# Layer 3 of a four-layer kernel: sums over states in four quarters of TensorE's array, and four of sixteen products du*B by TensorE

## The chip, the cores and the metric

The kernel runs on one core of a Trainium2 chip. Its time is the device time in microseconds of one execution, from the start to the end on that core. A core has five engines that run side by side, each with its own queue of instructions in a fixed order: TensorE (PE, matmuls from SBUF into PSUM), VectorE (DVE), ScalarE (ACT, activation functions), GpSimd (POOL) and SyncE (SP), which here issues nearly all DMAs.

## The reference, cut to what matters

Four layers work on eight images of 64 channels and 64 x 64 pixels. Layers 0 to 2 are not touched by the change. Layer 3 runs two directions of a Mamba block over one axis of the image, joins them by a linear map with a residual, and does the same over the other axis:

```python
def mamba1(x, nw, ipw, cw, cb, xpw, dtw, dtb, Alog, Dp, opw):
    xn = rms_norm(x, nw)
    xz = xn @ ipw.T                       # 64 -> 512
    xc, z = (xz[..., :d], xz[..., d:])    # d = 256
    xc = silu(causal_dwconv(xc, cw, cb))
    dbl = xc @ xpw.T                      # 256 -> 4 + 16 + 16
    dt = jax.nn.softplus(dbl[..., :r] @ dtw.T + dtb)
    Bm, Cm = dbl[..., r:r + n], dbl[..., r + n:r + 2 * n]
    A = -jnp.exp(Alog)
    y = selective_scan(xc, dt, Bm, Cm, A)
    return ((y + Dp * xc) * silu(z)) @ opw.T
# in selective_scan, for each step t of the sequence and each of n = 16 states:
    dA = jnp.exp(dt_t[:, :, None] * A)
    h = h * dA + (dt_t * x_t)[:, :, None] * B_t[:, None, :]
    y = jnp.einsum('bdn,bn->bd', h, C_t)
```

## The kernel before, in words

**Units and states.** Layer 3 is cut into 256 units: two axes (`s`), 16 chunks (`c`), four groups of eight sequences (`g`) and two directions (`k`; k=1 runs backwards). A unit has 512 tokens (eight sequences of 64). Its 256 channels lie as 128 partitions by two halves `j`, so that a tile is 128 x 1024 with the halves beside each other. For each of the 16 states n there is one pass over the tile. `stream` walks through all states of all units by one counter i (n = i modulo 16), and writes the order of every engine's queue out by hand: iteration i issues work for several states at once.

**What one state costs.** SP loads the rows of B and C of the state, spread over 128 partitions, into a tile `bc` six states ahead (L2068). POOL forms hb = du*B three states ahead (`multiply_b`, L484). ACT forms dA = exp(A*dt) in two halves two states ahead (`decay`, L491) into one of two PSUM tiles, in turn. DVE runs the scan h = dA*h + hb (`scan`, L500), in place in the PSUM tile of dA. Then h*C is formed (`multiply_c`, L514), for most states by DVE into a tile `hc`, for the states in the list `shared` by POOL, whose scan writes h to SBUF. PE adds the result to the unit's sum `acc` in PSUM, by matmuls with the identity (`gather`, L306), two iterations after the scan. `shared` has five states, or four in the k=1 units of odd g.

**Between units.** With state 0 of the next unit `gather` first lets DVE multiply the finished sum by z (`drain`, L2077), and PE then starts the next sum with D*u (`skip`, L2073). There is one tile `acc`. In iteration n=2 this stands behind the scan of state 2.

**Preparing the next unit.** `prepare` is a generator; `stream` runs one piece of it per iteration. Its pieces: PE forms px, the in-projection with the convolution's taps (L2012); ACT forms u = silu(px) (L2024); PE forms the 36 rows of dbl (L2027), ACT copies them out (L2030), SP stores the rows of B and C to HBM (L2033); PE forms dt's input (L2036), ACT dt = softplus (L415); POOL forms du = dt*u (L2047); PE forms z's input (L2050), ACT z = silu (L2060). Each matmul result stands in the PSUM tile `mm`, of which there is one (pool `pp`, one buffer), so that each waits for ACT to have read the one before.

**Other work in mm.** When both directions of a group are done, `finish` is queued as urgent: PE adds the residual and the four end products (L2096, L2099) in `mm`, and ACT copies them out (L2115). `begin` prepares a chunk of input, with the mean of squares in `mm`. `advance` runs their pieces where `room` allows it.

Of the kernel before, what the change touches and what calls it, by code (L numbers as in the profile page):

```python
# [10 lines left out]
F32 = mybir.dt.float32  # L11
# [7 lines left out]
C = 64  # L19
HW = 64  # L20
# [63 lines left out]
def twice(a):  # L84

    return np.concatenate([a, a], axis=0)
# [20 lines left out]
def layouts(i):  # L107
# [69 lines left out]
    o["l3_in"] = np.stack([twice(i[p + "in_proj_w"][k].T) for k in range(4)], axis=1)  # L177
# [6 lines left out]
    o["l3_xp"] = i[p + "x_proj_w"].reshape(4, 36, 2, 128).transpose(3, 0, 2, 1)  # L184
    o["l3_dtw"] = i[p + "dt_proj_w"].reshape(4, 256, 4).transpose(2, 0, 1)
# [3 lines left out]
    o["l3_out"] = i[p + "out_proj_w"].transpose(1, 0, 2)  # L189
# [73 lines left out]
def two(pool):  # L263


    return Ring([pool(f"pe{j}", 1, space=PSUM) for j in range(2)])


class Net:
# [33 lines left out]
    def mm(self, ps, lhsT, rhs, start=True, stop=True):  # L303

        for o, r in zip(blocks(like(ps, rhs)), blocks(rhs)):
            self.nc.tensor.matmul(o, lhsT, r, start=start, stop=stop)  # L306

# [124 lines left out]

    def stream(self, pools, ahead, steps, behind, rest=None):
# [30 lines left out]

        def fetch(i):
            if i < total and not isinstance(bp, tuple):
                s = steps[i // NS]
                t = bp.tile(s.bc_shape, F32, name="bc")
                s.load(i % NS, t)
                B[i], CC[i] = s.spread(t, 0), s.spread(t, 1)  # L470
            elif i < total:
                B[i] = bp[0].tile([128, T], F32, name="b")
                steps[i // NS].load(i % NS, 0, B[i])
# [5 lines left out]

        def multiply_b(i):  # L480
            if i < total:
                s = steps[i // NS]
                hb[i] = hbp.tile([128, T], F32, name="hb")
                nc.gpsimd.tensor_tensor(s.shaped(hb[i]), s.shaped(s.du), B.pop(i), ALU.mult)  # L484

        def decay(i):
            if i < total:
                s, n = steps[i // NS], i % NS
                dA[i] = pe.tile([128, T], F32, name="dA")
                for cut, A in s.lanes:  # L490
                    nc.scalar.activation(dA[i][:, cut], s.dt[:, cut], AF.Exp, scale=A[:, n : n + 1])  # L491

        def shared(i):
            return i % NS in steps[i // NS].shared

        def scan(i):
            s, n = steps[i // NS], i % NS
            h = hp.tile([128, T], F32, name="h") if shared(i) else dA[i]
            way = slice(None, None, -1) if s.rev else slice(None)
            nc.vector.tensor_tensor_scan(h[:, way], dA[i][:, way], hb.pop(i)[:, way], s.first(n), ALU.mult, ALU.add)  # L500
            dA[i] = h
            if shared(i):
                s.keep(n, h)

        def calm(i):

            return i + 1 >= total or not (shared(i) or shared(i + 1))
# [10 lines left out]
        def gather(i):  # L518
            at, n = divmod(i, NS)
            if n == 0:  # L520
                if at:
                    steps[at - 1].drain(acc.pop(at - 1))
                    steps[at - 1].done()
                acc[at] = pa.tile([128, T], F32, name="acc")
                begun[at] = steps[at].skip(acc[at])
            self.mm(acc[at], self.ident, hc.pop(i), start=n == 0 and not begun[at], stop=n == NS - 1)
# [12 lines left out]
        for i in range(total + 2):  # L539
            at, n = divmod(i, NS)  # L540
            need(i + ahead[0], "bc")
            need(i + ahead[1], "du")
            fetch_c(i + ahead[2])
            fetch(i + ahead[0])
            multiply_b(i + ahead[1])
            if 0 < i <= total and shared(i - 1):
                multiply_c(i - 1)


            first = i > NS and n == 2  # L550
            late = i > 1 and not first and steps[0].late and shared(i - 2)
            if i > 1 and not late and not first:
                gather(i - 2)
            if at + 1 < len(steps) and n == steps[at].start:
                steps[at + 1].ready()
                while self.held or self.urgent:
                    self.advance(behind)
                work = Task(steps[at + 1].prepare())
            if work is not None and not (self.held and work.said is None) and (calm(i) or not work.calm):
                work.step()  # L560
                if work.over:
                    work = None
            room = work is None or work.said is not True and (n < steps[0].early or hasattr(steps[at + 1], "du"))
            self.advance(behind, room, calm(i))
            if late:
                gather(i - 2)
            if i < total:
                scan(i)
            if first:
                gather(i - 2)  # L570
            if i < total:
                if not shared(i):
                    multiply_c(i)
            decay(i + 2)
# [292 lines left out]
    def layer1(self, src, dst):  # L867
        nc, tc, d = self.nc, self.tc, self.d
        mid = self.hbm["x1a"]
        with ExitStack() as ctx:  # L870
# [340 lines left out]
            class Step:  # L1211
                start, early, late = 2, 8, True
                shared = (1, 4, 7, 10, 13)
# [316 lines left out]
    def l2_scan(self, hx, hy):  # L1530
        nc, tc, d = self.nc, self.tc, self.d
        with ExitStack() as ctx:
# [36 lines left out]
            class Step:  # L1569
                bc_shape, start, early, late = [128, 2, T], 2, 0, False  # L1570
                shared = (1, 4, 7, 10, 13)
# [250 lines left out]
    def layer3(self, src, dst):  # L1822
# [8 lines left out]
        with ExitStack() as ctx:  # L1831
# [3 lines left out]
            pools = (pool("bc", 8), pool("hb", 4), pool("hc", 4), pool("h", 3), two(pool), pool("pa", 1, space=PSUM))  # L1835
            hp = pool("h3", 3, space=DRAM)
# [7 lines left out]
            class Weights:  # L1844
# [12 lines left out]
                def load(self):  # L1857
# [19 lines left out]
                    both = cp.tile([128, 2, 256], F32, name=f"both{s}")  # L1877
                    self.dtw, self.z = self.take("dtw", both[:4]), both[C:]
                    self.dtb, self.A, self.D = self.take("dtb"), self.take("A"), self.take("D")

                def build(self):
# [24 lines left out]
                    for k in range(2):  # L1906
                        nc.vector.tensor_scalar(
                            self.z[:, k, :], self.w_in[C:, k, 256:], self.nw[C:, k : k + 1], None, ALU.mult
                        )
# [14 lines left out]
            ends = [slice(3 + r, 3 + r + HW) for r in range(2)]  # L1924

# [58 lines left out]
            class Step:  # L1984
                bc_shape, start, early, late = [128, 2, W], 1, 0, False
# [5 lines left out]
                def __init__(self, s, c, g, k):  # L1991
                    self.s, self.c, self.g, self.k, self.rev = s, c, g, k, k == 1
                    self.w = weights[s]
                    self.shared = (2, 6, 10, 14) if k and g % 2 else (1, 4, 7, 10, 13)
                    self.lanes = [(slice(j * W, j * W + W), self.w.A[:, k, j, :]) for j in range(2)]
# [6 lines left out]
                def prepare(self):  # L2002
# [17 lines left out]
                    yield CALM  # L2020
# [4 lines left out]
                    pd = pp.tile([128, T], F32, name="mm")[:36, :W]  # L2025
# [3 lines left out]
                    dbl = p2.tile([36, W], F32, name="dbl")  # L2029
                    nc.scalar.copy(dbl, pd)  # L2030
                    self.bc = hp.tile([NS, 2, W], F32, name="bc")
                    for m in range(2):
                        nc.sync.dma_start(self.bc[:, m, :], dbl[4 + m * NS : 4 + m * NS + NS])  # L2033
                    pt = pp.tile([128, T], F32, name="mm")
                    for j in range(2):
                        nc.tensor.matmul(  # L2036
                            pt[:, j * W : j * W + W], w.dtw[:, k, j * 128 : j * 128 + 128], dbl[0:4], start=True, stop=True
                        )
                    yield True
                    yield CALM  # L2040
# [6 lines left out]
                    nc.gpsimd.tensor_tensor(du, dt, u, ALU.mult)  # L2047
                    pz = pp.tile([128, T], F32, name="mm")
                    for j in range(2):
                        nc.tensor.matmul(  # L2050
                            tokens(pz[:, j * W : j * W + W]),
                            w.z[:, k, j * 128 : j * 128 + 128],
                            xn[C:, :, 4 : 4 + HW],
                            start=True,
                            stop=True,
                        )
                    yield True
                    yield CALM
# [5 lines left out]
                    nc.scalar.copy(dt.rearrange("p (s t) -> p s t", t=HW)[:, :, at], endless)  # L2064

                def load(self, n, t):
                    row = self.bc[n : n + 1].rearrange("o m t -> o (m t)")
                    nc.sync.dma_start(t.rearrange("p m t -> p (m t)"), row.to_broadcast([128, 2 * W]))  # L2068

                def skip(self, acc):  # L2070
                    for j in range(2):
                        at = slice(j * W, j * W + W)
                        nc.tensor.matmul(acc[:, at], self.w.skip[self.k][:, j, :], self.u[:, at], start=True, stop=False)  # L2073
                    return True
# [83 lines left out]
```

## Time and profile before

| what | value |
|---|---|
| median of three runs | 24,507.96 us (24,494.8 to 24,517.75) |
| the profiled execution | 24,512.34 us, span 24,510.5 us, mean granted PE clock 0.939 |
| layer 3 in the profile | from 11,265 us to the end: 256 units, 51.7 us each |
| busy share, 20,000 to 24,000 us | PE 86%, DVE 97%, ACT 68%, POOL 99% |
| DMA busy share there | 0.52 of 16 engines |

A row of a group reads: line, engine, operation, output and inputs with shapes, count, then busy time in us and mean duration in ns, then idle time of the engine just before these instructions and what ended it. A row of the timeline reads: start, duration, engine, line, operation, count. Each f32 matmul shows as two records (two LDWEIGHTS and two MATMUL), in the timeline at 0.43 us from start to start for 512 columns at full clock. Durations of overlapping instructions overlap too, so start-to-start times are the ones that add up.

### The profile page before, as it was taken

The numbers are of one execution on the slowest core, as the hardware profiler recorded it, in microseconds if no ns is written. First come the engines' busy times: TensorE is split into PE (matmuls) and PEld (weight loads), VectorE is DVE, ScalarE is ACT, GpSimd is POOL, SyncE is SP. The second block draws the span as 40 slices with busy tenths as digits, with TensorE's granted clock in tenths as the row PEclk, the third lists the DMA queues.
The fourth block names the chain that finished last, engine by engine and source line by source line (L and its number), as shares of the span: only waits on it lengthen the run. The fifth ranks groups of instructions, "written<-read, shape, count | busy, mean of one in ns | idle before, by whom it ended". The sixth has DMA issues, their size and how long they took to land. (4 is left out here: it accounts for less than half of the span.)

```text
span 24510.5 us, 193203 instructions
## 1 busy us (share of the span) xinstructions
PE 20920.5 (85%) x53146; PEld 8078.3 (33%) x53146; DVE 22354.1 (91%) x13092; ACT 14737.2 (60%) x18960; POOL 22095.7 (90%) x10580
## 2 busy tenths in 40 slices
PE   7778888888888888898888888888888888888888
PEld 5323333333333223222333333333333333333333
DVE  5599999999998689978999999999999999999999
ACT  5445555555555456525666666666666666666666
POOL 0499999999999489967999999999999999999999
PEclk9889999999999999999999999999999999999999
DMA  3699889889888489924555555555555454555454
GB/s 78 203 327 321 312 313 322 314 313 320 313 313 309 171 287 339 317 54 121 172 169 172 170 172 169 170 170 172 170 170 173 169 174 167 173 170 172 168 174 157
DMA packets 1835294, 5282.70 MB, mean 216 GB/s; under 512 B 533712, under 2 KB 539924, under 8 KB 1831904
## 3 DMA queue, kind: packets, MB, share of 16 engines
q1 hardware_dynamic: 1809632, 5207.00, 62.8%
q10 hardware_dynamic: 24576, 63.33, 0.7%
q8 instruction: 423, 6.93, 0.1%
q14 instruction: 663, 5.43, 0.1%
HBM read 5112.85 MB, written 156.11 MB: 215 GB/s over the span
## 5 line engine op out<-in xcount | busy, mean ns | idle before, releaser
L484 POOL TENSOR_TENSOR hb<-du,bc 128x1024 f32<-128x1024 f32 x4608 | 10757.1, 2365 | 204.6 <-DVE h L500 144.3
L306 PE MATMUL acc<-hc,ident 128*128 128x512 f32 x18560 | 8783.6, 614 | 93.3 <-DVE img L1274 49.7
L491 ACT ACTIVATE dA<-dt,w_A 128x512 f32<-128x512 f32 x8192 | 5658.2, 691 | 3939.3 <-DVE hc L514 2886.0
L500 DVE TENSOR_TENSOR_SCAN dA<-dA,hb 128x1024 f32<-128x1024 f32 x3320 | 7579.3, 2283 | 195.4 <-ACT dA L491 105.2
L306 PE MATMUL acc<-h,ident 128*128 128x512 f32 x8064 | 4644.1, 705 | 2433.5 <-POOL h L514 2403.0
L306 PEld LDWEIGHTS acc<-hc,ident 128*128 128x128 f32 x18560 | 3639.8, 200 | 5218.0 <-issue 4534.5
L484 POOL TENSOR_TENSOR hb<-du,b 128x1024 f32<-128x1024 f32 x2048 | 4833.5, 2389 | 487.7 <-DVE dA L500 214.4
L514 DVE TENSOR_TENSOR hc<-dA,bc 128x1024 f32<-128x1024 f32 x3232 | 3956.5, 1224 | 246.0 <-issue 5.8
L491 ACT ACTIVATE dA<-dt,w_l_A 128x1024 f32<-128x1024 f32 x2560 | 2856.8, 1117 | 996.2 <-DVE hc L514 756.6
L500 DVE TENSOR_TENSOR_SCAN h<-dA,hb 128x1024 f32<-128x1024 f32 x1416 | 3228.9, 2280 | 79.9 <-ACT dA L491 77.8
L306 PEld LDWEIGHTS acc<-h,ident 128*128 128x128 f32 x8064 | 1565.6, 212 | 5153.0 <-POOL h L514 3477.1
L514 POOL TENSOR_TENSOR h<-h,bc 128x1024 f32<-128x1024 f32 x1376 | 3250.5, 2362 | 8.3 <-DVE h L500 8.3
L500 DVE TENSOR_TENSOR_SCAN dA<-dA,carry,hb 128x1024 f32<-128x1024 f32 x1320 | 3093.8, 2344 | 115.4 <-POOL hb L484 50.5
L514 DVE TENSOR_TENSOR hc<-dA,c 128x1024 f32<-128x1024 f32 x1408 | 1723.7, 1224 | 117.7 <-DMA c<-bc 5.1
L514 POOL TENSOR_TENSOR h<-h,c 128x1024 f32<-128x1024 f32 x640 | 1517.9, 2372 | 9.4 <-ACT carry L1257 8.6
L491 ACT ACT_TABLE_LOAD x1128 | 1447.2, 1283 | 19.9
L500 DVE TENSOR_TENSOR_SCAN h<-dA,carry,hb 128x1024 f32<-128x1024 f32 x600 | 1404.6, 2341 | 37.1 <-ACT dA L491 22.5
L1257 ACT COPY carry<-dA 128x1 f32<-128x1 f32 x1056 | 167.6, 159 | 1656.9 <-DVE hc L514 1614.0
L2012 PE MATMUL mm<-xn,taps 128*128 128x512 f32 x2048 | 933.7, 598 | 1.1 <-ACT z L2060 1.1
L2047 POOL TENSOR_TENSOR du<-dt,u 128x1024 f32<-128x1024 f32 x256 | 604.7, 2362 | 10.5 <-ACT dt L415 10.5
L2027 PE MATMUL mm<-u,w_xp 128*36 128x512 f32 x1024 | 492.9, 604 | 140.4 <-ACT u L2024 134.7
L726 POOL MEMSET xf<- 128x24 f32 x33 | 4.4, 143 | 639.9 <-PE ps L747 500.4
(320 smaller groups left out, 17894.1 us busy)
## 6 DMA issues: line engine op xcount, KB each, us to landing
bc<-bc SPq DMA_DIRECT2D x4096, 512.0 KB
b<-bc SPq DMA_DIRECT2D x2048, 512.0 KB
c<-bc SPq DMA_DIRECT2D x2048, 512.0 KB
bc<-bc SPq DMA_DIRECT2D x512, 1024.0 KB
tmp<-rs SPq DMA_DIRECT2D x93, 512.0 KB
raw<-x SPq DMA_DIRECT2D x64, 512.0 KB
inv<-rs SPq DMA_DIRECT2D x64, 512.0 KB
tmp<-x SPq DMA_DIRECT2D x192, 128.0 KB
```

The source lines that it names most:

```text
L306: self.nc.tensor.matmul(o, lhsT, r, start=start, stop=stop)
L484: nc.gpsimd.tensor_tensor(s.shaped(hb[i]), s.shaped(s.du), B.pop(i), ALU.mult)
L491: nc.scalar.activation(dA[i][:, cut], s.dt[:, cut], AF.Exp, scale=A[:, n : n + 1])
L500: nc.vector.tensor_tensor_scan(h[:, way], dA[i][:, way], hb.pop(i)[:, way], s.first(n), ALU.mult, ALU.add)
L514: engine.tensor_tensor(s.shaped(o), s.shaped(h), CC.pop(i), ALU.mult)
L726: nc.gpsimd.memset(x[:, :, HW:], 0.0)
L1257: nc.scalar.copy(self.carry[:, n : n + 1], h[:, last : last + 1])
L2012: nc.tensor.matmul(tokens(px[:, j * W : j * W + W]), w.taps[k][:, m, j * 128 : j * 128 + 128], xn[:, :, f : f + HW], start=m == 0, stop=m ...
L2027: nc.tensor.matmul(pd, w.xp[:, k, j, :], u[:, j * W : j * W + W], start=j == 0, stop=j == 1)
L2047: nc.gpsimd.tensor_tensor(du, dt, u, ALU.mult)
```

## The change

Only layer 3 changes; the instructions of layers 0 to 2 are the same.

**Sums in quarters.** `gather` calls `add_up`, which calls `quads`: instead of two matmuls of 128 x 128 by 512 there are four of 64 x 64 by 512, one for each pair of partition half r and channel half j. Each lies in another quarter of PE's array. In the sum the two halves change places: `acc` has channel half j on partition half j. The weights of z, of the out-projection and of skip are reordered on the host to fit. The two halves of dt's input and of z's input use different rows of the array as well, and `xp` gets 68 rows, so that dt's four stand on both partition halves.

**du*B by PE for states 2, 6, 10 and 14** (`direct`, `fed`). `prepare` ends with a new piece: PE transposes du by eight matmuls with the identity into `mm`, and ACT copies the result to SBUF (duT). The four rows of B are written by four new DMAs, element by element, onto the diagonals of 128 x 128 blocks in HBM (`diags`, cleared once at the start; row pitch 513 floats). For a fed state `load` fetches the diagonal blocks (256 KB) and the row of C (256 KB), two DMAs in place of one. `expand` multiplies duT by the blocks, in eight matmuls of 128 x 128 by 128, into `mm`; the scan reads hb from there. `expand(i + 1)` stands in iteration i. If a task holds `mm`, `expand` first runs the piece that frees it. For these states dA is formed by ACT into an SBUF tile of the pool `hb`, three states ahead.

**Products of h and C.** `shared` is now 2, 4, ... 14, in the k=1 units of odd g 0 as well: seven or eight states instead of five or four. Pool `hc` has three tiles instead of four.

**The order.** The pieces of `prepare` follow `plan`: px in iteration 3, u in 4, dbl and dt's input in 7, dt in 8, du in 9, z's input in 11, z in 12, the transposes in 15, the copy to duT in 0 of the next unit. `finish` and `begin` may take `mm` in iterations 0 and 12 (`rooms`). In the order that comes out on PE, `finish` stands in every k=0 unit but one between the sum of state 10 and the expand of state 14, and ACT's copy of it stands behind z; the mean of squares stands before the expand of state 2.

```diff
+    def quads(self, acc, lhsT, rhs, start=False, stop=False):
+        for r in range(2):
+            at = slice(r * C, r * C + C)
+            for j in range(2):
+                self.nc.tensor.matmul(
+                    acc[j * C : j * C + C, r * 512 : r * 512 + 512],
+                    lhsT(j)[at, at],
+                    rhs[at, j * 512 : j * 512 + 512],
+                    start=start, stop=stop,
+                )
...
         def multiply_b(i):
-            if i < total:
+            if i < total and direct(i):
+                dA[i] = hbp.tile([128, T], F32, name="hb")
+                exponents(i, dA[i])
+            elif i < total:
...
+        def expand(i):
+            if i < total and direct(i):
+                while self.held:
+                    self.release()
+                need(i, "duT")
+                hb[i] = steps[i // NS].expand(B.pop(i))
...
+            expand(i + 1)
             first = i > NS and n == 2
...
-            pools = (pool("bc", 8), pool("hb", 4), pool("hc", 4), pool("h", 3), two(pool), pool("pa", 1, space=PSUM))
-            hp = pool("h3", 3, space=DRAM)
+            pools = (pool("bc", 8), pool("hb", 4), pool("hc", 3), pool("h", 3), two(pool), pool("pa", 1, space=PSUM))
+            hp, hd = pool("h3", 3, space=DRAM), pool("hd", 1, space=DRAM)
...
+            fed = (2, 6, 10, 14)
+            diags = [hd.tile([len(fed), 128 * 513], F32, name=f"dg{e}") for e in range(2)]
...
-                bc_shape, start, early, late = [128, 2, W], 1, 0, False
+                bc_shape, start, early, late = [128, 2, W], 3, 0, False
+                direct, rooms = fed, (0, 12)
+                plan = {3: 1, 4: 1, 7: 2, 8: 1, 9: 1, 11: 1, 12: 1, 15: 1, 0: 1}
...
-                    self.shared = (2, 6, 10, 14) if k and g % 2 else (1, 4, 7, 10, 13)
+                    self.shared = (0, 2, 4, 6, 8, 10, 12, 14) if k and g % 2 else (2, 4, 6, 8, 10, 12, 14)
...
+                    for e, n in enumerate(fed):
+                        spots = self.diag[e : e + 1].rearrange("o (p x) -> o p x", x=513)[:, :, :W]
+                        spots = spots.rearrange("o p (m y) -> o m p y", y=128)[:, :, :, 0]
+                        nc.sync.dma_start(spots, dbl[4 + n : 5 + n].rearrange("o (m p) -> o m p", p=128))
...
+                    px = pp.tile([128, T], F32, name="mm")
+                    for m in range(T // 128):
+                        at = slice(m * 128, m * 128 + 128)
+                        nc.tensor.matmul(px[:, at], du[:, at], net.ident, start=True, stop=True)
+                    yield True
+                    self.duT = p1.tile([128, T], F32, name="duT")
+                    nc.scalar.copy(self.duT, px)
+
+                def expand(self, diag):
+                    hb = pp.tile([128, T], F32, name="mm")
+                    for j in range(2):
+                        for m in range(4):
+                            at = slice(j * W + m * 128, j * W + m * 128 + 128)
+                            nc.tensor.matmul(hb[:, at], self.duT[:, at], diag[:, m * 128 : m * 128 + 128], start=True, stop=True)
+                    return hb
```

## The prediction

> **What bounds the kernel now.** I read the groups by line from 11,000 us on (layer 3 starts at 11,265), then busy time by stretch, then the timeline of single units.
>
> ```profile
> L484 POOL TENSOR_TENSOR hb<-du,bc 128x1024 f32<-128x1024 f32 x4096 | 9559.5, 2365 | 167.3 <-DVE h L500 130.9 <-DVE dA L500 35.6 <-DMA bc<-bc 0.3
> L514 POOL TENSOR_TENSOR h<-h,bc 128x1024 f32<-128x1024 f32 x1216 | 2873.2, 2363 | 5.8 <-DVE h L500 5.8
> L514 DVE TENSOR_TENSOR hc<-dA,bc 128x1024 f32<-128x1024 f32 x2880 | 3525.7, 1224 | 219.5 <-issue 4.9 <-PE mm L2027 0.4 <-DMA bc<-dbl 0.4
> ...
> 20000.00:24000.00 4000.00, 3456.13 (x7286) 1315.97 (x7285) 3884.53 (x2201) 2702.95 (x3583) 3950.97 (x1727) 0.96 0.52 171
> ```
>
> The last row is PE, PEld, DVE, ACT, POOL busy: POOL 98.8%, DVE 97.1%, PE 86%, ACT 68%, DMA share 0.52. Layer 3 has 256 units in 13,230 us: 51.7 us each. POOL and DVE are both full; a gain needs both shortened.
>
> ```profile
> 16024.02 9.32 POOL L484 TENSOR_TENSOR hb<-du,bc 128x1024 f32<-128x1024 f32 x4
> 16044.71 2.29 DVE L500 TENSOR_TENSOR_SCAN dA<-dA,hb 128x1024 f32<-128x1024 f32 x1
> 16047.03 1.22 DVE L514 TENSOR_TENSOR hc<-dA,bc 128x1024 f32<-128x1024 f32 x1
> 16048.17 2.28 DVE L500 TENSOR_TENSOR_SCAN h<-dA,hb 128x1024 f32<-128x1024 f32 x1
> 16050.36 2.27 DVE L500 TENSOR_TENSOR_SCAN dA<-dA,hb 128x1024 f32<-128x1024 f32 x1
> ```
>
> Start to start: a POOL product 2.33; a scan with its hc product 2.33+1.14 = 3.48; a scan whose product is POOL's 2.19. POOL does 16+4.75+1 products a unit: 50.7, with xn 51.4. That is the 51.7.
>
> **POOL and DVE after.** Four states leave POOL (16 to 12), shared products rise from 4.75 to a mean 7.25: 20.25 x 2.33 + 0.7 = 47.9. DVE: 7.25 x 2.19 + 8.75 x 3.48 + 1.14 (z) = 47.5 (48.0 with seven shared, 46.9 with eight). Without new waits a unit takes about 48.2: 3.5 x 256 = 900 us gained.
>
> **PE's load.**
>
> ```profile
> 10435.97 1.08 PE L403 MATMUL ps<-sum,ident 64*64 64x512 f32 x8
> 62.77 1.05 PE L634 MATMUL pt<-w_cent,x 128*128 128x128 f32 x8
> 16042.23 3.60 PE L2012 MATMUL mm<-xn,taps 128*128 128x512 f32 x8
> 16072.67 1.08 PE L2096 MATMUL mm<-raw,w_res 64*64 64x512 f32 x2 [0.66 <-ACT z L2060]
> 16073.69 3.65 PE L2099 MATMUL mm<-z,w_end 128*64 128x512 f32 x8
> ```
>
> A 128x512 matmul is two records of 0.43. Four quarter blocks (L403, eight records) take 0.86 start to start, as two full matmuls took 1.72: the quarters overlap. An expand, eight 128x128x128 products, is 16 records of 0.11: 1.9. Between shapes the next matmul starts 0.6 after the last instead of 0.43 (the L2096 row: 1.02 for two). Per unit: sums 27.5 to 13.8; skip, dt and z save 2.6; expands add 7.6, transposes 1.9, some 16 switches 3. The load falls by about 4. What counts is where the expands stand.
>
> **The new waits.** All small products, the expanded hb included, share one PSUM tile "mm". expand(n) must wait until the last reader of mm is done, and DVE's scan(n) waits for expand. I follow one unit by hand, with durations from the groups by line (ACT: table load 1.28; two exponentials 1.42; u or dt 1.27; z 1.03; out 0.91; dbl 0.58).
>
> State 6, from scan 2 at 0: z ends 3.4; skip, the sums of 0 and 1 (3 x 0.86), then px (3.6 with the switch's wait) end at 9.9; u on ACT 11.3; expand to 13.3. DVE has z and scans 3, 4, 5 with two hc: wants scan 6 at 12.5. Stall 0.8.
>
> State 10, from scan 6: sums, pd 4.4, dbl 5.1, but dt on ACT stands behind the exponential of state 9, which waits for hc 7 (5.7): dt ends 9.8, expand 11.9; wanted 11.4. Stall 0.5.
>
> State 14, from H, the end of hc 11: the exponential of state 13 reuses 11's PSUM buffer, so it runs to H+1.5; table and z to 3.85. In the k=1 units expand follows: 5.9 against a wanted 5.7. In the k=0 units (127 of 128 in the order of PE) the finish of the pair before stands between: res and four end products 4.65 (the two rows above), ACT's out 0.9, only then expand: H+11.7. Stall 6.0. Before, finish held mm too, but no scan read mm.
>
> State 2: duT is ready about 2 us ahead; no stall. (Twice in eight units the mean of squares stands in mm before this expand, some 3 us: 1 us past the slack, 0.3 a unit, within the error.)
>
> At full PE clock: k=0 units 48.0+0.8+0.5+6.0 = 55.3; k=1 47.5+0.8+0.5+0.2 = 49.0; mean 52.2, +0.5 a unit.
>
> **The clock.** Row first:
>
> ```profile
> 16022.79 3.78 PE L306 MATMUL acc<-h,ident 128*128 128x512 f32 x4 [4.62 <-POOL h L514]
> ...
> 16085.29 2.98 PE L306 MATMUL acc<-h,ident 128*128 128x512 f32 x4 [2.61 <-POOL h L514]
> ```
>
> Such a group of four takes 1.98 on a warm PE. In ten timelines of 100 us, groups after a gap of 3.3 us or more took 2.5 to 3.8, all 12; of those under 2 us none did. The weight loads of the first row stay slow for 5 us. [...] The change has two such gaps on its critical chains: before skip (the sum of state 15 is done about 4 us before z) and before the sum of state 10 (pz ends H-2.2, POOL's product at H+1.8, as du stands before it). [...] I take 1.7 at state 6, and at state 14 1.4 (k=0) and 1.1. Units: 58.4 and 51.7; mean 55.1.
>
> **The rest.** No row has a scan that reads its second operand from PSUM; the nearest, z (acc in PSUM, 1.21) against hc (1.22), shows no difference: 0, between -0.1 and +0.1 each, at most 0.4 a unit. The hc tiles go from four to three; hc 5 reuses the tile of hc 0, summed 4 us before: 0 while PE keeps that lead. ACT gains the duT copy (1.03 as z): 32% idle hides it. SP issues 26 DMAs a unit instead of 18, at 0.3 to 1 us: hidden; late loads would show on POOL. The four scatters of B to the diagonals are 512 pieces of 4 bytes each.
>
> ```profile
> DMA packets 576, 0.13 MB, mean 26 GB/s; under 512 B 576, under 2 KB 576, under 8 KB 576
> ...
> hm<-so SPq DMA_DIRECT2D x8, 16.0 KB
> ```
>
> [...] No row has 4-byte stores. [...] Loads 14 and 15 queue behind them; from dbl there are about 10 us before hb 15 delays anyone. [...] Clearing the diagonals, 2.1 MB once at some 300 GB/s: 7 us. Layers 0 to 2 issue the same instructions.
>
> Sum: (55.1 - 51.7) x 256 = 870; +7; against the profiled 24,512 (span 24,510.5), 4 above the median: 25,385, say 25,390.
>
> **Rivals.**
> Hidden waits, faster: POOL's and DVE's relief decides if the stalls stay below 51.7 - 47.5 - 0.5 = 3.7 us a unit on average. Full relief gives 23,610; half of it 24,060. For it: balanced saturated engines and PE 14% idle. Against: 6 us at state 14 in every second unit is a chain of dependent instructions, 3.0 in the mean alone, and needs no contention.
> Warm clock, same waits: 52.2, so 24,630.
> [...]
> Quarters that do not overlap would be 64 x 0.86 = 55 us of sums: PE-bound, over 70 us a unit. The L403 row speaks against it; under 2 in 100.
>
> **Chances.** Late expands with cold PE 0.46 (own range 25,000 to 25,900); warm 0.16; slow scatters or serial quarters 0.16; hidden 0.22, of which 0.18 faster and 0.04 near even. About 0.2% (49 us) is what a measurement can tell; the warm case also touches it. Faster 0.18, same 0.05, slower 0.77. The range, 24,350 to 26,900, leaves out full relief and the slowest scatters.
>
> **What would show it.** After: POOL below 92% busy; DVE scans of hb in mm idle before expand, most at state 14 beside ACT's out; expand waiting for ACT; PE clock under 0.92 in layer 3. If the expand's wait is a DMA on bc, scatters are the cause; if DVE stays above 95% busy, I am wrong.

## The result, and the profile after

The changed kernel takes 26,307.0 us (median of four, 26,295.6 to 26,343.0), the kernel before 24,512.9 beside it: a ratio of 1.0735, 95% interval 1.0716 to 1.0754. The profiled execution spans 26,314.1 us. The forecast was 25,390: the direction is right and the time lies in the range, but the loss is 1,794 us where 877 were forecast.

Layer 3 still starts at 11,265 us, so a unit takes (26,314 - 11,265) / 256 = 58.8 us instead of 51.7, against a forecast of 55.1. First the busy times of 20,000 to 24,000 us (PE, PEld, DVE, ACT, POOL, then the granted clock, the DMA share, GB/s):

```profile
20000.00:24000.00 4000.00, 3049.81 (x16650) 1408.89 (x16650) 3252.45 (x1780) 2452.24 (x3257) 3291.72 (x1431) 0.84 0.50 152
```

POOL fell from 98.8 to 82.3%, DVE from 97.1 to 81.3%, the clock from 0.96 to 0.84. Nobody is full any more. The groups of layer 3 by line tell where the time went (busy, mean ns | idle before, releasers):

```profile
L526 POOL TENSOR_TENSOR hb<-du,bc 128x1024 f32<-128x1024 f32 x3072 | 7213.5, 2355 | 1330.0 <-DVE h L548 565.0 <-DMA bc<-bc 383.1 <-DVE dA L548 380.9
L562 POOL TENSOR_TENSOR h<-h,bc 128x1024 f32<-128x1024 f32 x1856 | 4372.0, 2356 | 1236.9 <-DVE h L548 1233.9 <-issue 2.9
L548 DVE TENSOR_TENSOR_SCAN h<-hb,mm 128x1024 f32<-128x1024 f32 x1024 | 2340.1, 2285 | 2708.5 <-PE mm L2151 2708.4
L2193 PE MATMUL mm<-z,w_end 128*64 128x512 f32 x1016 | 762.5, 921 | 0.0
```

POOL has the 12 products a unit of hb and the 7.25 of C that were forecast. It idles mostly because DVE is late (383 us of its waits are for loads; e7_once below shows what they are worth), and DVE is late in front of one kind of instruction: the 1,024 scans that read the expanded hb in mm wait 2,708 us for the expand, 10.6 us a unit. No other group of DVE waits 300 us. The finish's end products take 921 ns a record where the kernel before took 598:

```profile
L2099 PE MATMUL mm<-z,w_end 128*64 128x512 f32 x1016 | 463.2, 598 | 0.0
```

One k=0 unit, from the scan of state 10 to that of state 14 (rows left out are marked by dots):

```profile
20046.88 2.29 DVE L548 TENSOR_TENSOR_SCAN h<-hb,mm 128x1024 f32<-128x1024 f32 x1 [1.82 <-PE mm L2151]
...
20049.50 1.14 PE L2123 MATMUL mm<-xn,both 64*128 64x512 f32 x4
...
20053.28 1.98 PE L320 MATMUL acc<-h,ident 64*64 64x512 f32 x8 [2.63 <-POOL h L562]
...
20055.37 1.02 ACT L2132 ACTIVATE z<-mm 128x1024 f32<-128x1024 f32 x1
...
20056.45 1.96 PE L2190 MATMUL mm<-raw,w_res 64*64 64x512 f32 x2 [1.19 <-ACT z L2132]
20057.09 1.23 DVE L562 TENSOR_TENSOR hc<-dA,bc 128x1024 f32<-128x1024 f32 x1
20058.35 6.13 PE L2193 MATMUL mm<-z,w_end 128*64 128x512 f32 x8
...
20064.51 0.69 ACT L2209 ACTIVATE out<-mm,w_l_linb 64x512 f32<-64x512 f32 x1 [8.01 <-PE mm L2193]
...
20065.25 2.05 PE L2151 MATMUL mm<-bc,duT 128*128 128x128 f32 x16 [0.78 <-ACT out L2209]
...
20067.34 2.29 DVE L548 TENSOR_TENSOR_SCAN h<-hb,mm 128x1024 f32<-128x1024 f32 x1 [9.03 <-PE mm L2151]
```

This is the forecast chain, link by link: z, res and end products, ACT's out, expand, scan. Only the two matmul groups of the finish take 8.0 us (20,056.45 to 20,064.48) where 4.65 were their warm time. The granted clock, the third number from the end in the next row, is half from ahead of the first group nearly to the end of the second, long after the gap:

```profile
20053.20:20063.30 10.10, 8.83 (x16) 2.02 (x17) 5.02 (x3) 3.24 (x5) 8.49 (x5) 0.50 0.55 210
```

State 10 in the same unit:

```profile
20039.91 1.09 PE L320 MATMUL acc<-h,ident 64*64 64x512 f32 x8
...
20042.12 1.26 ACT L435 ACTIVATE dt<-mm,w_dtb 128x512 f32<-128x512 f32 x2
...
20043.43 3.41 PE L2151 MATMUL mm<-bc,duT 128*128 128x128 f32 x16 [2.43 <-ACT dt L435]
...
20046.88 2.29 DVE L548 TENSOR_TENSOR_SCAN h<-hb,mm 128x1024 f32<-128x1024 f32 x1 [1.82 <-PE mm L2151]
```

dt ends 9.8 us after scan 6 (20,033.62), as forecast to the tenth. PE sat idle for 2.43 us, and then the expand took 3.41 instead of 2.05.

Below, a stall is read from DVE's timeline: the start of a scan, less the start of the instruction before it, less the usual spacing of such a pair. Means over the 205 units that begin between 12,000 and 24,000 us, in us:

| scan of state | forecast | measured | with the gap filled |
|---|---|---|---|
| 6 | 0.8 warm + 1.7 = 2.5 | 1.9 (k=0), 2.4 (k=1) | not filled |
| 10 | 0.5 | 2.1 to 2.2 | 0.5 (e12_ten) |
| 14, k=0 (finish between) | 6.0 warm + 1.4 = 7.4 | 9.25 | 6.0 (e15_finish) |
| 14, k=1 | 0.2 warm + 1.1 = 1.3 | 2.0 | 0.3 (e15_finish) |
| 2 | 0 | 1.0 | not filled |
| mean of a unit | 7.35 | 10.9 | |

Without stalls a unit is 47.4 us, against a forecast of 47.5 to 48.0.

### The profile page after: what moved, and what is told of

Same layout as the page of the kernel before. It is cut to its first block, busy times and chain, and to the rows that moved or that the text cites. A ratio compares the mean times of both kernels' runs of the same rounds, so it can differ in the third digit from the quotient of the medians.

```text
span 26314.1 us, 269765 instructions
## 1 busy us (share of the span) xinstructions
PE 20900.9 (79%) x91034; PEld 8980.3 (34%) x91034; DVE 21635.3 (82%) x12456; ACT 14937.9 (57%) x19247; POOL 21321.8 (81%) x10196
## 5 line engine op out<-in xcount | busy, mean ns | idle before, releaser
L526 POOL TENSOR_TENSOR hb<-du,bc 128x1024 f32<-128x1024 f32 x3584 | 8410.1, 2355 | 1363.4 <-DVE h L548 573.8
L562 POOL TENSOR_TENSOR h<-h,bc 128x1024 f32<-128x1024 f32 x2016 | 4748.4, 2355 | 1238.7 <-DVE h L548 1235.6
L548 DVE TENSOR_TENSOR_SCAN h<-hb,mm 128x1024 f32<-128x1024 f32 x1024 | 2340.1, 2285 | 2708.5 <-PE mm L2151 2708.4
L2151 PE MATMUL mm<-bc,duT 128*128 128x128 f32 x16384 | 2850.8, 345 | 1459.0 <-ACT dt L435 621.0
L310 PE MATMUL acc<-hc,ident 128*128 128x512 f32 x7040 | 3386.5, 618 | 88.4 <-DVE img L1328 51.9
L2151 PEld LDWEIGHTS mm<-bc,duT 128*128 128x128 f32 x16384 | 2618.1, 251 | 2408.4 <-ACT dt L435 845.8
L320 PE MATMUL acc<-hc,ident 64*64 64x512 f32 x17920 | 2787.6, 706 | 0.8 <-DVE hc L562 0.8
L320 PE MATMUL acc<-h,ident 64*64 64x512 f32 x14848 | 2173.4, 658 | 769.0 <-POOL h L562 756.0
L310 PE MATMUL acc<-h,ident 128*128 128x512 f32 x3200 | 1878.5, 717 | 862.7 <-POOL h L562 836.3
L310 PEld LDWEIGHTS acc<-hc,ident 128*128 128x128 f32 x7040 | 1396.9, 202 | 2094.8 <-issue 1717.0
```

Source lines behind the costliest of these rows:

```text
L320: self.nc.tensor.matmul(acc[j * C : j * C + C, r * 512 : r * 512 + 512], lhsT(j)[at, at], rhs[at, j * 512 : j * 512 + 512], start=start, s ...
L548: nc.vector.tensor_tensor_scan(h[:, way], dA[i][:, way], b[:, way], s.first(n), ALU.mult, ALU.add)
L562: engine.tensor_tensor(s.shaped(o), s.shaped(h), CC.pop(i), ALU.mult)
L2151: nc.tensor.matmul(hb[:, at], self.duT[:, at], diag[:, m * 128 : m * 128 + 128], start=True, stop=True)
```

## The experiments

Medians; all ratios are to the kernel before, run beside each on the same chip. Its medians there lie between 24,507 and 24,528 us, so a difference of some 20 us between two rows tells nothing. "Won" means less than the 26,307 us of the changed kernel.

| run | us | ratio, 95% interval |
|---|---|---|
| after | 26,307 | 1.0735 (1.0716 to 1.0754) |
| e1_warm | 25,622 | 1.0448 (1.0432 to 1.0464) |
| e12_ten | 25,929 | 1.0579 (1.0565 to 1.0593) |
| e15_finish | 25,825 | 1.0532 (1.0517 to 1.0546) |
| e2_late | 25,831 | 1.0532 (1.0514 to 1.0549) |
| e3_px | 25,901 | 1.0562 (1.0547 to 1.0578) |
| e4_plain | 26,816 | 1.0936 (1.0919 to 1.0952) |
| e13_quads | 24,519 | 1.0000 (0.9991 to 1.0008) |
| e9_none | 25,746 | 1.0504 (1.0490 to 1.0518) |
| e10_one | 26,080 | 1.0642 (1.0627 to 1.0656) |
| e11_two | 25,284 | 1.0315 (1.0301 to 1.0329) |
| e8_three | 25,759 | 1.0511 (1.0496 to 1.0527) |
| e7_once | 26,219 | 1.0698 (1.0682 to 1.0714) |
| e14_mean | 26,243 | 1.0704 (1.0689 to 1.0718) |
| e5_moved | 25,262 | 1.0309 (1.0294 to 1.0325) |
| e6_all | 25,244 | 1.0305 (1.0288 to 1.0322) |
| e16_best | 25,183 | 1.0269 (1.0255 to 1.0283) |
| e17_mid | 24,765 | 1.0109 (1.0092 to 1.0125) |

**Is it the slow clock? All gaps filled (e1_warm), one gap (e12_ten), the gaps around the finish (e15_finish).** A group of four 64x64 matmuls with a zero block, added into acc, keeps PE busy (1.04 us a group in e12_ten, the first row of its timeline below) without changing a value (this diff and those below are shortened; where a finish stands ahead of state 14's expand, the group goes ahead of the finish alone):

```diff
+    def warm(self, n):
+        for _ in range(n if self.live is not None else 0):
+            for r in range(2):
+                at = slice(r * C, r * C + C)
+                for j in range(2):
+                    self.nc.tensor.matmul(
+                        self.live[j * C : j * C + C, r * 512 : r * 512 + 512],
+                        self.zero[at, at], self.still[at], start=False, stop=False)
...
                 need(i, "duT")
+                self.warm({10: 2, 14: 1, 2: 1}.get(i % NS, 0))   # e12_ten: {10: 1}; e15_finish: {14: 1}
...
+            if n == 10:
+                self.warm(2)                                     # ahead of the sum of state 10; not in e12_ten
             steps[at].add_up(...)
...
+                net.warm(1)                                      # in finish(); not in e12_ten
```

> The change, with idle gaps of TensorE filled: matmuls of a zero weight block into acc (they add nothing) before the expand of states 10 (two groups of four), 14 and 2 (one), before the sum of state 10 (two) and before the finish (one). Theory A (the waits are the forecast ones and a slow TensorE clock in the gaps made them longer): the stall before the scan of state 10 falls from 2.1 to 0.5 us, of state 14 from 9.2 to 5.8 in the k=0 units and from 2.0 to 0.4 in the k=1 units, of state 2 from 1.0 to 0.5: 4.6 us a unit, 1,180 us, so about 25,130. Theory B (the stalls are the places of ACT's and PE's instructions in their queues; the clock has little to do with it): the added matmuls are only more work, 26,300 to 26,500.

> The change with one group of four matmuls of a zero block added ahead of the expand of state 10, and none elsewhere: the gap of 2.4 us before that expand becomes about 1.4. Theory A (the gap alone makes the expand slow): the expand takes 2.05 instead of 3.65 us in all units, the stall of state 10 falls from 2.1 to 0.5, 1.6 x 256 = 410 us less, 25,900. Theory B (what is won at state 10 comes back at state 14 or 2): less than 200 us.

> The change, with matmuls of a zero block before the sum of state 10 (two groups of four), the finish (one) and the expand of state 14 in units without a finish (one); none at state 10's expand. Theory A (the finish's ten products and that expand are slow after a gap): the stall of state 14 falls from 9.2 to 6.2 in the k=0 units and from 2.0 to 1.0 in the k=1 units, 2.0 us on average, 510 us, 25,800. Theory B (POOL's and ACT's places end the wait): less than 200 us.

e12_ten won 378 us, forecast 410 by theory A. Of its timeline, one expand of state 10:

```profile
20031.26 1.04 PE L334 MATMUL acc<-taps,zero 64*64 64x512 f32 x8
20033.87 2.05 PE L2175 MATMUL mm<-bc,duT 128*128 128x128 f32 x16 [1.58 <-ACT dt L449]
20035.96 2.29 DVE L564 TENSOR_TENSOR_SCAN h<-hb,mm 128x1024 f32<-128x1024 f32 x1 [0.47 <-PE mm L2175]
```

The expand waits for the same dt, 1.58 us after PE's last work instead of 2.43, and takes 2.05 us: so in 210 of 210 units from 12,000 to 24,000 us, where all 205 of the changed kernel were slow (mean 3.68). The granted clock during the expand, in the changed kernel and here:

```profile
20043.43:20046.30 2.87, 2.87 (x13) 2.87 (x14) 1.53 (x2) 2.83 (x4) 2.87 (x3) 0.50 0.12 4
20033.87:20035.92 2.05, 2.05 (x20) 1.93 (x22) 1.53 (x2) 2.00 (x3) 2.05 (x2) 1.00 0.12 1
```

The scan of state 10 now stalls 0.55, the forecast's warm figure.

e15_finish won 482 us, forecast 510. Its groups of the finish, from 11,300 to 24,500 us:

```profile
L2219 PE MATMUL mm<-z,w_end 128*64 128x512 f32 x920 | 419.4, 598 | 0.0
L2216 PE MATMUL mm<-raw,w_res 64*64 64x512 f32 x230 | 124.8, 622 | 148.4 <-ACT z L2156 148.4
```

598 and 622 ns a record are the times of before. The stall of state 14 is 6.0 us in the k=0 units and 0.3 in the others, where the forecast had 6.0 and 0.2 for a warm PE. The two runs together are worth 860 us; e1_warm, with both and more, won 685 instead of 1,180. Its states 10 and 14 fell nearly as foretold (0.55; 6.45 and 1.05), but state 2 rose from 1.0 to 1.4 and state 15 from 0.1 to 0.4 on average. In each of the three runs states 2, 6 and 15 together take 0.7 to 0.9 us a unit back. So the slow clock is shown as the cause at states 10 and 14, and a part of what is won there comes back at other states.

**Where the finish and px stand (e2_late, e3_px, e5_moved).**

```diff
+            if plan and n == 15 and not self.held:     # e2_late: behind scan 14, ahead of the transposes
+                self.urgent[0].step(); self.held = self.urgent
...
+            elif plan and n == 0 and self.held:
+                self.release()
```
```diff
             if first:
+                work = Task(steps[at + 1].prepare())   # e3_px: px, then z drain, skip, sums
+                work.step()
                 gather(i - 2)
```

> The change, with the finish of a pair moved from between the sum of state 10 and the expand of state 14 to behind the scan of state 14 (before the transposes). Theory A (the finish between costs 7.2 us in every second unit, 3.4 of them because its ten matmul records run at half clock): the stall of state 14 in the k=0 units falls from 9.2 to 2.0, state 2 of the next unit gains 1 to 4, since transposes now wait for the finish: 3 to 6 us in 128 units, so 25,550 to 25,900. Theory B (the finish merely fills a wait that another chain ends, z on ACT): under 100 us, 26,200 or more.

> The change, with the px product issued ahead of skip and the first two sums of a unit instead of behind them. Theory A (the wait of state 6 is the chain z, skip, sums, px, u, expand with a slow clock at its start): the stall of state 6 falls from 2.0 to between 0 and 0.5 us, 380 to 510 us less, so about 25,850. Theory B (the later skip and sums hold the three hc tiles and the accumulator, a new wait of the same size comes): 26,200 to 26,500, with DVE waiting for PE before hc products.

> The change, with px ahead of skip, and with both the finish and the mean of squares issued behind the scan of state 14 (no matmuls added to fill gaps). Theory A (each stall is its own chain through mm, and they add): of the 11.0 us of stalls a unit, state 6 falls from 2.1 to 0.8, state 14 from a mean of 5.6 to 2.0, state 10 stays at 2.1 (its expand is still cold), state 2 stays near 1: 4.9 us less, 25,060. Theory B (stalls replace each other: what is taken from one state comes back at the next): less than the 880 us that the two moves gave alone, above 25,430.

e2_late won 476 us, within what theory A expected. In three quarters of the units state 14 stalls 2.0; in the rest it is 6.7, since the mean of squares, which shares the places, moved there. State 2 rose from 1.0 to 1.6. e3_px won 406, within theory A too, though state 6 fell from 2.1 to 0.8 only; no wait came at the hc tiles. e5_moved, with both and with the mean moved too, won 1,045, more than the 882 of the two single moves: the stalls do add as theory A has it, but it missed 25,060 by 200, since state 2 rose to 1.6 and one unit in eight still had 7.7 at state 14.

**The quarters by themselves (e4_plain, e13_quads, e9_none).**

```diff
                 def add_up(self, acc, hc, start, stop):
-                    net.quads(acc, lambda j: net.ident, hc, start, stop)
+                    net.plain_sum(acc, hc, start, stop)     # e4_plain
```
```diff
-            self.mm(acc[at], self.ident, hc.pop(i), ...)     # e13_quads: kernel before
+            self.quads(acc[at], lambda j: self.ident, hc.pop(i), ...)
```
```diff
-            fed = (2, 6, 10, 14)
+            fed = ()                                         # e9_none; transposes left out,
+            direct, rooms = fed, (12,)                       # finish and mean in iteration 12 alone
```

> The change, with the sums and skip made as before by full 128x128 identity blocks (0.86 more PE time each), and the expands kept. Theory A (thin PE work costs clock): gaps shrink by 0.9 and more stay under 2 us; the expand of state 10 is warm (-1.6), the finish partly (-2 in every second unit), state 6 pays 2.6 for three longer groups and saves 1.7 by a warm px: about -1.7 us a unit, 25,900. Theory B (only PE's load counts): every chain with sums in it is longer: 2.6 at state 6, 0.9 each at states 10 and 14: 26,700 to 27,500.

> The kernel before with one part of the change alone: sums over states and skip in four quarters (with the reordered rows of z and of the output projection), all else as before, every du*B on POOL. Theory A (PE was not the bound, and no scan waits for PE): 24,510, within 60 us. Theory B (the thinner PE's slow clock costs by itself): slower by 100 us or more. Theory C (PE's 14 us a unit were in the way of POOL and DVE): faster by 100 us or more.

> The change with no fed state: sums and skip in quarters, but every du*B on POOL, the lists of POOL's C products as before, no transposes, scatters or expands. Theory A (only scans that wait for mm are hurt by a slow clock, and POOL bounds the unit): POOL's 51.4 us a unit as before, 24,510, within 60 us either way. Theory B (the thinner PE costs time by itself): 100 to 500 us slower, 24,600 to 25,000. A third (PE's load was in the way before): 24,400 and below.

e13_quads is level with the kernel before, within a tenth of a per cent. Its busy times in the stretch shown above:

```profile
20000.00:24000.00 4000.00, 2825.11 (x12568) 756.13 (x12560) 3883.67 (x2201) 2705.32 (x3584) 3949.13 (x1726) 0.80 0.53 171
```

PE is busy 71 instead of 86%, at a clock of 0.80, lower than in the changed kernel, and POOL and DVE are as full as before. In the order of before, quarters cost nothing and win nothing, and the slow PE does no harm. In e4_plain the mean granted clock of the whole execution is 0.943, where the changed kernel has 0.875 and the kernel before 0.939, and state 10 stalls 1.1 us, but the chains with sums in them are longer (3.4 us at state 6 in the k=0 units and 5.0 in the k=1 units, 4.1 and 0.7 at state 2): 509 us slower than the change, against theory A and within theory B. With expands in the path, shorter sums are worth 2 us a unit.

e9_none met none of its three theories. With no scan reading mm it should have fallen back to 24,510 and stayed at 25,746. Its waits of DVE, then of ACT (us in total, times, longest), 12,000 to 24,000 us:

```profile
DVE dA L548 <- ACT dA L517: 932.0, 448, 5.2
DVE h L548 <- ACT dA L517: 172.6, 76, 3.1
...
ACT out L2202 <- PE mm L2186: 585.0, 107, 6.4
...
ACT u L2091 <- PE mm L2080: 300.2, 212, 3.3
```

The change also wrote a new order of the small products (the plan), with u, dt, z and out between the exponentials. Here scans wait 5.2 us a unit (1,105 us over 213 units) for exponentials that stand on ACT behind u and out, which wait for PE. In e13_quads, with the order of before and a clock nearly as low (0.80 against 0.77), DVE waits 129 us for exponentials in the same stretch and ACT's out 61 us for PE. So the loss of 1,227 us between these two kernels comes with the new order. That the order alone makes it isn't shown: the finish is slow in all 107 units of e9_none looked at (7.0 us on average instead of 4.65), and no run has the new order, no fed state and a warm PE. (e9_none also has three hc tiles instead of four, for which DVE waited 0.4 us in all, and the inputs of dt and z in halves of the array.) In the changed kernel this cost doesn't show, as DVE waits for an exponential only 2.7 us in 12,000: its waits stand at the mm scans.

**How many states to feed (e10_one, e11_two, e8_three).** `fed` is (2,), (2, 6) with px first, and (2, 6, 10); the first two have five and six C products on POOL, and finish and mean in iteration 12 alone.

> The change with one fed state, 2, whose expand has some 2 us of slack, and five of POOL's C products in each unit; the finish and the mean of squares only after the sum of state 10. Theory A (a fed state is worth having where mm is free early): POOL 15 + 5 + 1 products and 0.7, 49.6 us; DVE 5 x 2.19 + 11 x 3.48 + 1.14 = 50.4; a stall of 0 to 1 at state 2: 50.4 to 51.4 us a unit, 24,180 to 24,440, faster than the kernel before. Theory B (any scan that reads mm pulls the chain of PE and ACT into the path): a stall over 1.3 us at state 2, 24,510 or more.

> The change with two fed states, 2 and 6, six of POOL's C products in each unit, and px ahead of skip. Theory A: POOL 14 + 6 + 1 products and 0.7, 49.6 us; DVE 6 x 2.19 + 10 x 3.48 + 1.14 = 49.1; stalls of 0.7 at state 6 and 0 to 1 at state 2: 49.8 to 50.9, 24,030 to 24,310. Theory B (a second fed state costs more than its 1.3 us of DVE and POOL): above the kernel with one fed state.

> The change with three fed states (2, 6, 10); state 14 goes back to POOL. Theory A (stalls of DVE bound the unit, POOL has room): the stall of state 14, 5.6 us on average, goes, POOL's 50.2 us still fit: 58.8 - 5.6 = 53.2 us a unit, about 24,880. Theory B (POOL's relief matters as much as the stall): the added product counts in full, 55.5 us a unit, 25,470.

None met theory A, and none came out by the cause that theory B names. e10_one has no stall at all at state 2, but 1,401 us of waits for ACT's exponentials in 12,000 us. e11_two waits 909 us for ACT and 168 for the expand; with px moved as well, it is faster than e10_one. e8_three lost the wait for the expand at state 14 and won 548 us where theory A expected 1,430: 714 us of waits for ACT came in its place, at states 14 and 15. The exponentials of a fed state go to SBUF and not through the ring of two PSUM tiles; that fewer fed states bring the ACT waits back by this is argued, not shown.

**Smaller suspects (e7_once, e14_mean).** e7_once leaves out most scatters (later units use an early unit's B), and e14_mean leaves out the mean of squares (one channel's square stands for it).

```diff
-                    for e, n in enumerate(fed):
+                    for e, n in enumerate(fed if self.c + self.g == 0 else ()):   # e7_once
```
```diff
-                    self.mm(ps[:1, :], mean, sq)                                   # e14_mean
-                    nc.scalar.copy(ms, ps[:1, :])
+                    nc.scalar.copy(ms, sq[:1, :])
```

> The change, with the scatters onto the diagonals made only in the 16 units of the first chunk of each half for g=0; later units reuse those diagonals, so B of the four fed states is that of an early unit. Theory A (the scatters lie beside other work, but late loads cost DVE about 0.2 us a unit at state 15): 0 to 100 us less, 26,200 to 26,310. Theory B (the scatters are part of the loss): 300 us less or more, 26,000 and below.

> The change, with the mean of squares of layer 3 left out of TensorE (the square of channel 0 stands for it), so that nothing but the transposes stands in mm ahead of state 2's expand. Theory A (the stall of state 2, 1.0 us a unit on average, is the mean's): 250 us less, 26,050. Theory B (state 2 waits for POOL's du and the loads): less than 80 us.

e7_once won 88 us, as theory A had it: the scatters are nearly hidden. POOL's waits for loads of hb fell from 383 to 44 us, so these waits were worth 88 us at most. e14_mean won 64, under theory B's bound. State 2's stall fell from 1.0 to 0.4 a unit, but 0.3 came back at states 0 and 1: once in eight units DVE now waits 3 to 4.5 us in sum for the reciprocal's input, an exponential and POOL's hb.

What is left at state 2, 3 to 4 us once in eight units, can be followed in the changed kernel's trace. These rows are of one such unit:

```profile
16720.48 1.40 POOL L2040 TENSOR_TENSOR xn<-raw,inv 128x560 f32<-128x560 f32 x1 [5.79 <-DMA inv<-rs]
...
16728.85 1.99 PE L320 MATMUL acc<-h,ident 64*64 64x512 f32 x8 [6.00 <-POOL h L562]
...
16737.49 2.29 DVE L548 TENSOR_TENSOR_SCAN h<-hb,mm 128x1024 f32<-128x1024 f32 x1 [2.67 <-PE mm L2151]
```

POOL waits for the rows of inv before the first xn product of a chunk, so its product of h and C is late, the sum on PE waits for that, and the transposes, duT and the expand stand behind the sum. In all 26 units of this kind POOL waits so, 6.3 us on average. In e17_mid, where xn comes five pieces later, this wait of POOL is gone and at most 2 us of the stall are left; other things changed there too.

**Can four fed states win (e6_all, e16_best, e17_mid)?** e6_all is e5_moved with the gaps filled; e16_best adds z one state earlier (`11: 2` in the plan), loads seven ahead, xn later; e17_mid puts finish and mean directly behind pz.

> The same moves with the idle gaps of TensorE filled by matmuls of a zero block (before the expands of states 10, 14 and 2 and the sums of states 10 and 15). Theory A: on top of the moves, state 10 falls from 2.1 to 0.5, state 14 from 2.0 to 1.0, state 2 stays near 1: 2.6 us a unit less than the moves alone, 51.3 us a unit, 24,400, just under the kernel before. Theory B (the filled gaps and the moves win the same time): within 150 us of the moves alone.

> The four fed states with px ahead of skip, finish and mean behind the scan of state 14, z one state earlier, loads one state further ahead, the xn products five pieces later, and zero-block matmuls before the expand and the sum of state 10 only. Theory A (each stall can be moved off): about 0.5, 0.5, 0.7 and 1.5 us at states 6, 10, 14 and 2: 50.7 us a unit, 24,250, faster than before. Theory B (POOL and PE, both in order, hand the delay on): 52.5 to 54 us a unit, 24,700 to 25,100.

> As the kernel with all places changed, but finish and mean stand directly behind pz, ahead of the sum of state 10 (which waits for POOL), and one group of zero-block matmuls instead of two stands before that sum. Theory A (the finish only needs a place where nothing late stands ahead of it): from scan 10, z ends at 5.8 us, finish 10.5, out 11.4, expand 13.5 against a wanted 11.4: a stall of 2 to 3 at state 14 in the k=0 units in place of 6 to 9 at state 2, 51.5 to 52 us a unit, 24,450 to 24,600, level with the kernel before. Theory B (the products of the finish are slow or ACT's out is late wherever it stands): 5 us or more at state 14, above 24,800.

e6_all won nothing beyond e5_moved: state 10 gave 1.4 us, and state 2 took 1.5 back, since the finish behind scan 14 waits on PE for the sum of POOL's product of state 12. e16_best has only 0.7, 0.55 and 0.3 us at states 6, 10 and 14, but 1.1 at state 13 behind the earlier z and 3.8 on average at state 2 (from 0 to 11), where finish and transposes share mm; it is slower than both of its theories had it. e17_mid takes the finish out of there, and most units have nothing left at state 2:

```profile
DVE h L564 <- PE mm L2187: 735.1, 668, 5.4
DVE dA L564 <- ACT dA L531: 296.1, 267, 4.2
```

That is 3.2 us for PE and 1.3 for ACT a unit (12,000 us hold 228 units) instead of 10.6: 24,765 us, above the 24,450 to 24,600 expected. 1,542 of the 1,794 us are won back by order, earlier loads and filled gaps; no version here beats the kernel before.

## Where the prediction held, and which step failed

- **Bound, POOL's and DVE's relief: right.** 47.4 us a unit without stalls against 47.5 to 48.0; POOL at 82%, under the 92% named.
- **Where the stalls come: right.** They stand before scans of hb in mm, most at state 14 beside ACT's out. The warm chains were right to 0.1 us where a gap was filled: 0.5 at state 10, 6.0 and 0.3 at state 14.
- **The clock: the step that failed, by size.** The prediction allowed nothing for a slow PE at state 10 and 1.25 us a unit (1.4 in the k=0 units, 1.1 in the k=1 units) at state 14. The runs with filled gaps show 1.6 and 2.5: 2.85 of the 3.5 us by which a unit was set too low. No run shows the 1.7 us taken at state 6 nor the 1.4 and 1.1 at state 14; they were the author's estimate. In their place the runs showed 3.25 us (k=0) and 1.7 (k=1) at state 14 (e15_finish), and at state 6 a whole stall of 1.9 and 2.4 us.
  - State 10: the prediction read from before that groups after gaps of 3.3 us or more are slow and those under 2 us not, and left 2 to 3.3 us open. It then counted a gap only before skip and before the sum of state 10. The gap ahead of state 10's expand, 2.4 us while dt stands behind an exponential, lay in the open zone and got nothing. It costs 1.6 us in every unit (e12_ten: 378 us). The trace of before did not support that. The second of the two rows shown has a gap of 2.61 us and is slow, and over layer 3 of before 75 of the 157 groups of four sums after a gap of 2 to 3.3 us took more than 2.4 us.
  - State 14: at the finish it took +1.4, a slow spell of few microseconds. The finish was slow in every one of 102 units, 8.0 us on average (end and residual products, (762.5 + 249.5) / 127) instead of 4.65: +3.25 in the k=0 units. In the k=1 units it is +1.7 where 1.1 was taken (e15_finish: 482 us for both).
- **State 6** was taken at 2.5 and measured 2.1, the one stall set too high. How much of it is the clock was not run.
- **State 2 was set at 0** (0.3 for the mean of squares "within the error"); it is 1.0. Leaving the mean out of PE takes 0.6 of it: in one unit of eight the expand behind the mean is slow too, 3.78 us instead of 2.05, which the prediction did not count. The rest is the chain from POOL's wait for inv, which the prediction did not follow.
- The sum of these: 55.1 + 1.65 (state 10) + 1.25 (state 14, mean of both) + 1.0 (state 2) - 0.4 (state 6) - 0.3 (base) + 0.2 (small waits) = 58.5, against a measured mean of 58.6 for the 205 units.
- **Scatters, serial quarters, reading hb from PSUM**: rightly left out. Without most scatters the time falls by 88 us (e7_once). The eight records of a sum in quarters take 1.09 us (the L320 row of state 10 above); one after the other, at the 0.43 us a record of before, they would be 3.4. The scans of hb in mm take 2,285 ns, the others 2,277. Clearing the diagonals took 10.1 us, 11,236.0 to 11,246.1 us in the changed kernel's trace, where 7 were forecast at some 300 GB/s (the page of before has 309 to 327 GB/s in eleven slices of the layers ahead of layer 3); layer 3 starts no later for it.
- **The rival of hidden waits** would have decided below 3.7 us a unit; the stalls are 10.9.
- **Not foreseen**: that with no scan reading mm the new order still loses 5%, in waits for ACT (e9_none). The prediction checked DVE's waits on PE, not what ACT's order costs once they are gone.

## What to carry to other kernels

When an operand of the saturated engine moves to another engine, follow for each use the buffer that it passes through, to the last reader before it, and add the queue positions on every engine in between; as long as that chain doesn't fit, the freed throughput can be lost in it, as it was here, in stalls of 10.9 us a unit. When PE's work gets thinner, cost the critical products behind its gaps at the slow clock, and with them the whole run of products that follows: here an expand took 3.68 us instead of 2.05 behind a gap of 2.4 us, and the finish 8.0 instead of 4.65. When a stall is removed, ask which engine ends the next wait: in e8_three, e9_none and e10_one the waits that came were for ACT.

## What the runs showed of the hardware

- After an idle gap of 2.4 us the expand of state 10 was slow in 205 of 205 units of the changed kernel, 3.68 us on average; after one of 1.6 us it took 2.05 us in 210 of 210 units of e12_ten.
- The length of the gap alone does not decide. In the changed kernel, ahead of state 2, a gap of 2.31 us was followed by a slow expand (over 2.4 us) in 65 of 77 units, and one of 1.09 us, behind the mean of squares, in 25 of 50.
- In the changed kernel's trace, all 1,335 changes of the granted clock between 12,000 and 24,000 us lie within 0.01 us of one grid of 3.41 us, and the 451 in the trace of before as near to a grid of the same step. Counted on that grid, in the trace of before, a stretch at full clock in which PE's records cover under 40% was followed by one at half clock in 182 of 182 cases, and one with 45% or more in 0 of 2,923. From half clock it went back to full after 223 of 223 stretches with 85% or more, and after 0 of 114 with less than 80%. In the changed kernel's trace the borders are less sharp: 118 of 1,820 stretches with 45% or more were followed by half clock, and 74 of 735 at half clock with 85% or more were not followed by full clock. Why is not shown.
- A slow spell can last: in the k=0 unit shown, the clock is at half from 20,053.1 to 20,063.4 us, three steps of this grid, though PE is idle for only 1.3 us in it.
- A low clock cost nothing in e13_quads: at 0.80 from 20,000 to 24,000 us it takes 24,519 us, level with the kernel before beside it (24,518), whose clock there is 0.96.
- The four scatters of 512 four-byte pieces hold the issuing queue for some 6.4 us a unit, 1,631 us in the changed kernel's trace; without most of them (e7_once) the time fell by 88 us.
